# Tail of a decoder layer on one core: routers paired, the last tile's router fed from raw tokens, loads moved to another queue

## The chip, the cores and the metric

The kernel runs on one core of a Trainium2 chip. The metric is the device time of one execution in microseconds (us); the number compared is the median of several runs. TensorE multiplies matrices into PSUM; VectorE (DVE), ScalarE (ACT) and GpSimd (POOL) work elementwise; SyncE (SP) only starts DMA transfers. ScalarE can start DMA transfers as well, from its own queue, and they stand there in order with its other instructions.

## The reference

There are 2048 tokens (32 sequences of 64) of width 512, everything in float32. Three sublayers with residuals:

```python
x = x + attn(layernorm(x))      # 32 heads of 128, RMS norm of q and k, output weights Wo (4096 x 512)
x = x + xattn(layernorm(x))     # 64x64 weights, context of 128 columns, a softmax, and a skip product
x = x + ffn(layernorm(x))
# ffn, with flat = layernorm(x), 64 experts, 8 chosen:
logits = flat @ router_weight.T + router_bias
scores = softmax(logits)
topk_w, topk_idx = top_k(scores, 8)
w_dense = zeros.at[arange(T)[:, None], topk_idx].add(topk_w)
out = flat * topk_w.sum(-1, keepdims=True) + w_dense @ expert_bias
```

## The kernel before, in words

The 2048 tokens are 16 tiles of 128. In a first phase TensorE makes the queries, keys and values of two heads at a time and half of the tokens (32 groups, by a Strassen scheme on two levels), and the mixed values of each group go to DRAM (`mixed`). In the second phase the output product with Wo runs over eight pairs of tiles, again by Strassen: seven products of 32 matmul records each (16 blocks of 128 rows in float32; every record is a 128x256 product). `chunks` (L879) yields after every 4 blocks, that is after 8 records, and after every yield `advance()` runs one step of the work that follows: each tile that has its attention output has a generator `after_attention`, made of `cross_attention` and `experts`, and `yield n` in it lets n further calls of `advance()` pass before its next step. At an `advance()` the tiles take their steps in the order of their numbers. A tile's steps in `cross_attention`: load of the context tile `ct` and layernorm (L1087); `kv` (L1094); the energies `e` and the softmax (L1105 to L1139); the transposes of the probabilities (L279, copies L1144); the skip product (L1114) and the mixtures (L1149), added to x (L1158). In `experts`: layernorm; transposes of the normed tile and a copy to `ft` (L1168); the logits `pl` with `ft` as the stationary operand and the 64 router columns moving (L1173); softmax and choice of eight on VectorE and ScalarE (L1178 to L1205); the weights turned (L1212); the product with the expert biases `pm` (L1222), the last addition (L1225) and the store (L1226). Tiles 2p and 2p+1 already share the turned weights (`wds` of both beside each other); tiles 14 and 15 go alone.

The order on TensorE is the order of the code throughout. On VectorE, ScalarE and GpSimd it is the order of the code up to the end of the first phase (`ordered.close()`), and is planned by the framework after it, from priorities and estimated times. A tile of a pool waits until the buffer of its tag is free; `att` and `ft` have one buffer each.

After the last product TensorE has nothing but tiles 14 and 15 left. There `fill(n)` puts n transposes of the identity into TensorE's queue, after the steps that the table `FILL` names. From the loop over the pairs, pair 7 calls `advance()` a second time behind chunks 8, 12, 16 and 18, and at its end `while tails: advance()` runs the rest.

In the last group of the first phase, a plan of 4 x 4 steps (`plan` in `double`, filled by `also(n, m, ...)`) also holds the first loads of the output product: `load_wo` (L851) with two transfers of 1 MB a call, from SP's queue at the start of the group and from ScalarE's at step (1, 0), and the mixtures of tiles 0 and 1 (L863) at steps (2, 0) to (2, 2). The same queue of SP carries the norms' factors: `row_w` out (L652), `rs` back in as a broadcast (L563), from which `scale` (L574 on VectorE, L572 on GpSimd) works.

Of the kernel before, what the change touches and what calls it, by code (L numbers as in the profile page):

```python
# [41 lines left out]
def decoder_layer(  # L42
# [182 lines left out]
    def fill(count):  # L225
# [8 lines left out]
        (NT - 1, "keys"): 18,  # L234
        (NT - 2, "mixtures"): 18,
# [610 lines left out]
    def load_wo(k, n, places, queue):  # L846

        halves = []
        for i, it in enumerate(places):
            it = it.rearrange("p (g f) -> p g f", f=DH)  # L850
            queue.dma_start(  # L851
                out=it,
                in_=wo.rearrange("(g k p) f -> k p g f", k=HG, p=HD)[
                    k, :, i * KH : (i + 1) * KH, bass.ts(n, DH)
                ],
            )
            halves.append(it)
        return halves
# [225 lines left out]
    def cross_attention(t, xt, apart):  # L1084
# [5 lines left out]
        nc.sync.dma_start(out=ct, in_=ctx_flat[bass.ts(t, P), :])  # L1090
# [27 lines left out]
        py = skip() if t == NT - 1 else None  # L1118
        probs = []
        for b in range(2):  # L1120
# [4 lines left out]
            nc.vector.tensor_scalar(neg, mx, -(SEQ**-0.5), None, ALU.mult)  # L1125
# [20 lines left out]
        yield 2  # L1146
# [12 lines left out]

    chosen_by = {}  # L1160

    def experts(t, xt):
        name = f"f{t}"
        xn = layernorm(xt, name)

        yield 8 if t == NT - 2 else 3
        ft = work.tile([P, KC, P], F32, tag="ft", name=f"ft_{name}", bufs=1)
        nc.scalar.copy(ft, transposed(xn.rearrange("p (kc k) -> p kc k", k=P), name))  # L1168
        fill_behind(t, "router's input")
        yield 1  # L1170
        pl = ps_s.tile([P, NEXP], F32, tag="ps", name=f"pl_{name}")
        for kc in range(KC):
            nc.tensor.matmul(  # L1173
                pl, ft[:, kc, :], rwt[:, kc, :], start=kc == 0, stop=kc == KC - 1
            )
        fill_behind(t, "router")
        lg = work.tile([P, NEXP], F32, tag="lg", name=f"lg_{name}")
        nc.vector.tensor_tensor(lg, pl, rb_b, ALU.add)  # L1178
        top = small.tile([P, 8], F32, tag="top", name=f"top_{name}")
        nc.vector.max(top, lg)  # L1180
        neg = small.tile([P, 1], F32, tag="neg", name=f"neg_{name}")
        nc.vector.tensor_scalar(neg, top[:, 0:1], -1.0, None, ALU.mult)
        ex = work.tile([P, NEXP], F32, tag="ex", name=f"ex_{name}")
        den = small.tile([P, 1], F32, tag="den", name=f"den_{name}")
        nc.scalar.activation(ex, lg, AF.Exp, bias=neg, accum_out=den)
        inv = small.tile([P, 1], F32, tag="inv1", name=f"inv1_{name}")
        nc.vector.reciprocal(inv, den)

        rest = work.tile([P, NEXP], F32, tag="rest", name=f"rest_{name}")
        nc.vector.match_replace(rest, top, lg, -3e38)  # L1190
        chosen = work.tile([P, NEXP], F32, tag="chosen", name=f"chosen_{name}")
        nc.vector.tensor_tensor(chosen, lg, rest, ALU.not_equal)

        alone = t >= NT - 2
        side = 0 if alone else t % 2
        if side:
            wds, other = chosen_by.pop(t - 1)
        else:
            wds = work.tile([P, 2, NEXP], F32, tag="wds", name=f"wds_{name}")
        wd = wds[:, side, :]  # L1200
        nc.vector.scalar_tensor_tensor(wd, ex, inv, chosen, ALU.mult, ALU.mult)
        ws = small.tile([P, 1], F32, tag="ws", name=f"ws_{name}")
        nc.vector.tensor_reduce(ws, wd, AX.X, ALU.add)

        nc.vector.scalar_tensor_tensor(xt, xn, ws, xt, ALU.mult, ALU.add)  # L1205
        if not alone and not side:
            chosen_by[t] = wds, xt
            return
        yield 3
        n = NEXP if alone else 2 * NEXP  # L1210
# [434 lines left out]
```

## Time and profile before

| what | us |
|---|---|
| median of 3 runs | 1870.45 (1868.06 to 1873.12) |
| the profiled execution | 1869.75 |
| its span, first to last instruction | 1868.0 |
| TensorE busy (matmul) | 1850.4 |
| VectorE busy | 1245.1 |
| GpSimd busy | 1014.7 |
| ScalarE busy | 653.6 |
| last product with Wo ends | 1841.1 |
| `fill` in the whole span | 76 transposes |

Times in the timeline count from the first instruction of the span. A group of instructions is given as start, length, engine, line, out<-in and count; "PEld" is the loading of the stationary operand, which overlaps the products. A float32 matmul appears as two records. The granted TensorE clock was 0.999 of full speed over the span.

### The profile page before, as it was taken

Reading aid. Unit: us, or ns where it says so; the run is one execution under the profiler, and the core shown is the slowest. Engines: PE = TensorE matmul, PEld = TensorE weight load, DVE = VectorE, ACT = ScalarE, POOL = GpSimd, SP = SyncE. Lnnn points to the kernel's source line nnn. Section 1 sums busy time; section 2 is a strip of 40 time slices with the busy share of each in tenths; the row PEclk is TensorE's granted clock in tenths of the full one; section 3 lists DMA queues with packets and bytes.
Section 4 is the critical chain, followed back from the end, with each engine's and each line's share of the span. In section 5 each row is a group of like instructions: output and inputs, shape, how many; then the busy total and the mean of one; then the engine's idle time right before and its main releaser. Section 6 shows DMA issues by size and latency. Waiting matters only on the chain.

```text
span 1868.0 us, 40676 instructions
## 1 busy us (share of the span) xinstructions
PE 1850.4 (99%) x16914; PEld 1616.9 (87%) x16914; DVE 1245.1 (67%) x2110; ACT 653.6 (35%) x1577; POOL 1014.7 (54%) x852
## 2 busy tenths in 40 slices
PE   9999999999999999999999999999999999999999
PEld 8888998898899888898889988988888888788876
DVE  6877777777666758777667767766684445554555
ACT  2344444444433443434443343444312202221222
POOL 4866777776667639776667777766242121212120
PEclk9999999999999999999999999999999999999999
DMA  4234434433443343333343333334944231223100
GB/s 143 69 122 144 134 125 131 131 109 110 131 136 114 114 139 112 109 109 103 130 134 123 109 110 114 103 115 141 312 122 159 91 116 68 71 94 116 46 26 23
DMA packets 164650, 215.06 MB, mean 115 GB/s; under 512 B 10161, under 2 KB 135153, under 8 KB 160369
## 3 DMA queue, kind: packets, MB, share of 16 engines
q1 hardware_dynamic: 157648, 206.62, 34.2%
q10 hardware_dynamic: 6816, 5.83, 1.0%
q8 instruction: 133, 2.18, 0.5%
q14 instruction: 53, 0.43, 0.1%
HBM read 172.05 MB, written 40.37 MB: 114 GB/s over the span
## 4 chain that ended last, share of the span: by engine, by line
PE 88%; DVE 4%; DMA 3%; POOL 3%; ACT 1%; issue 1%; SPq 0%; ACTq 0%; POOLq 0%; DVEq 0%
PE p_w L685 32%; PE py L879 17%; PE va L417 11%; PE vb L417 8%; PE o L622 3%; PE s L585 3%; PE ms_w L821 3%; PE pt_p L279 1%; PE pa L475 1%; PE e_x L1105 1%; PE py_x L1149 1%; PE pt_x L279 1%; POOL w L120 1%; PE pl_f L1173 1%; PE py_x L1114 1%; PE pb L475 1%
## 5 line engine op out<-in xcount | busy, mean ns | idle before, releaser
L685 PE MATMUL p_w<-x,w 128*128 128x256 f32 x2940 | 721.1, 382 | 2.5 <-DVE qk L696 1.7
L685 PEld LDWEIGHTS p_w<-x,w 128*128 128x128 f32 x2940 | 521.4, 190 | 59.3 <-DVE qk L696 1.2
L417 PEld LDWEIGHTS va<-w,x 128*128 128x128 f32 x2048 | 268.6, 192 | 13.0
L696 DVE TENSOR_TENSOR qk<-p_w,qk 128x512 f32<-128x512 f32 x360 | 213.1, 599 | 94.6 <-PE p_w L685 92.3
L433 ACT COPY v<-va 128x256 f32<-128x256 f32 x256 | 96.2, 376 | 497.5 <-PE va L417 497.5
L417 PE MATMUL va<-w,x 128*128 128x128 f32 x2048 | 269.9, 275 | 0.0
L709 DVE TENSOR_TENSOR qk<-p_w,qk 128x512 f32<-128x512 f32 x360 | 220.5, 620 | 46.5 <-PE p_w L685 43.1
L120 POOL TENSOR_TENSOR w<-w 128x768 f32<-128x768 f32 x126 | 249.7, 1993 | 2.4
L572 POOL TENSOR_TENSOR qk<-qk,rs 128x512 f32<-128x512 f32 x128 | 173.0, 1352 | 111.8 <-DMA rs<-row_w 99.4
L295 POOL TENSOR_TENSOR prob<-prob,inv 128x512 f32<-128x512 f32 x64 | 79.2, 1237 | 281.5 <-DVE inv L294 278.3
L879 PE MATMUL py<-wo,a 128*128 128x256 f32 x992 | 227.2, 382 | 0.0
L386 ACT ACTIVATE sq<-qk 128x512 f32<-128x512 f32 x256 | 161.4, 631 | 183.6 <-DVE qk L709 64.4
L879 PEld LDWEIGHTS py<-wo,a 128*128 128x128 f32 x992 | 184.1, 190 | 32.9 <-issue 8.6
L417 PEld LDWEIGHTS vb<-w,x 128*128 128x128 f32 x1536 | 201.3, 192 | 9.7
L417 PE MATMUL vb<-w,x 128*128 128x128 f32 x1536 | 202.4, 275 | 0.0
L574 DVE SCALAR_TENSOR_TENSOR qk<-qk,gqk,rs 128x512 f32<-128x512 f32 x128 | 164.7, 1287 | 3.8 <-DMA rs<-row_w 3.5
L879 PE MATMUL py<-wo_t,a 128*128 128x256 f32 x672 | 155.1, 382 | 0.0
L879 PEld LDWEIGHTS py<-wo_t,a 128*128 128x128 f32 x672 | 124.3, 190 | 18.2 <-issue 1.6
L1003 POOL TENSOR_TENSOR x<-x,p 128x256 f32<-128x256 f32 x42 | 42.9, 1043 | 166.7 <-ACT p L1056 72.2
L437 DVE TENSOR_TENSOR v<-vb,v 128x256 f32<-128x256 f32 x192 | 80.9, 421 | 57.0 <-ACT v L433 28.8
L765 POOL TENSOR_TENSOR qk<-qk 128x256 f32<-128x256 f32 x120 | 102.8, 857 | 10.5 <-DVE qk L709 5.8
L287 DVE TENSOR_REDUCE mx<-s 128x8 f32<-128x512 f32 x64 | 44.1, 689 | 85.4 <-PE s L585 85.3
(197 smaller groups left out, 2253.7 us busy)
## 6 DMA issues: line engine op xcount, KB each, us to landing
rs<-row_w SPq DMA_DIRECT2D x120, 512.0 KB
mixed<-ot SPq DMA_DIRECT2D x64, 512.0 KB
a<-mixed SPq DMA_DIRECT2D x32, 1024.0 KB
w<-in_wq_dram SPq DMA_DIRECT2D x64, 256.0 KB
w<-in_wk_dram SPq DMA_DIRECT2D x62, 256.0 KB
w<-in_wv_dram SPq DMA_DIRECT2D x62, 256.0 KB
x<-in_x_dram SPq DMA_DIRECT2D x20, 256.0 KB
rs<-row SPq DMA_DIRECT2D x8, 512.0 KB
```

Source lines behind the costliest of these rows:

```text
L120: on.tensor_tensor(*(it.rearrange("p c j d -> p (c j) d") for it in (out, a, b)), ALU.subtract)
L386: nc.scalar.activation(sq, of, AF.Square)
L417: nc.tensor.matmul(to[:, j, :], left[i][:, c, j, :], right[i][:, c, 2, :], start=first and j == 0 and c == 0, stop=c == 1, skip_group_chec ...
L433: nc.scalar.copy(self.v[h, ab], what)
L437: nc.vector.tensor_tensor(it, what, it, ALU.add)
L572: nc.gpsimd.tensor_tensor(k, k, rk, ALU.mult)
L574: lambda: nc.vector.scalar_tensor_tensor(q, q, gqk, rq, ALU.mult, ALU.mult)
L685: nc.tensor.matmul(bank[:, s, :], self.w.inner[o][i], inner_x[self.half, o][i], start=first and s == 0, stop=True, skip_group_check=True,)
L696: nc.vector.tensor_tensor(to(t, j), bank, add(t, j), ALU.add)
L709: nc.vector.tensor_tensor(to(t, j), bank, to(t, j), ALU.add)
L765: on.tensor_tensor(to, to, what, ALU.add)
L879: nc.tensor.matmul(py, a[:, g, :], b[g // KH][:, g % KH, :], start=n == 0 and g == 0, stop=n == last and g == NHG - 1,)
```

## The change

- Tiles 0 to 13: the even tile makes its `ft` and stops; with the odd tile's the router weights become the stationary operand (64 columns for each of the two tiles, in the two column halves of the array) and the tokens move. The logits of both tiles come out turned, are copied and transposed back, and both tiles' choices are made in one step. `ft` of two tiles lies in one buffer, that of `att`.
- Tile 15: its raw tokens are transposed before the norm's factors are known. The router weights, centred by their column means (`centre`, called by tile 14), take the mean's place, and the logits are multiplied by `rstd`. The copy to `ft` is shared by ScalarE and VectorE, and `xn` is made on GpSimd. The expert weights are not divided by the softmax sum; the factor comes in with the last addition, which is made in two halves, each with its own product and its own store, on SP's and ScalarE's queue.
- Tile 14: its mixtures come one `advance()` earlier (`yield 1`), and with them all its later steps; its x is scaled and added to on GpSimd.
- `FILL`: 18 after tile 15's keys go, 18 after tile 14's mixtures become 2, 22 after tile 15's energies are new.
- Tile 15's negated maxima are made on ScalarE.
- The context tiles of tiles 0 and 1 are loaded from ScalarE's queue.
- The first four Wo loads are issued one by one from ScalarE's queue, at steps (0, 2), (1, 0), (1, 2) and (1, 3) of the last group.

```diff
     FILL = {
-        (NT - 1, "keys"): 18,
-        (NT - 2, "mixtures"): 18,
+        (NT - 2, "mixtures"): 2,
+        (NT - 1, "energies"): 22,
...
-        nc.sync.dma_start(out=ct, in_=ctx_flat[bass.ts(t, P), :])
+        (nc.scalar if t < 2 else nc.sync).dma_start(out=ct, in_=ctx_flat[bass.ts(t, P), :])
...
+        fill_behind(t, "energies")
...
-            nc.vector.tensor_scalar(neg, mx, -(SEQ**-0.5), None, ALU.mult)
+            if t == NT - 1:
+                nc.scalar.mul(neg, mx, -(SEQ**-0.5))
+            else:
+                nc.vector.tensor_scalar(neg, mx, -(SEQ**-0.5), None, ALU.mult)
...
-        yield 2
+        yield 1 if t == NT - 2 else 2
...
+    def centre():
+        mean_of = work.tile([P, P], F32, tag="wt", name="mean_of")
+        nc.gpsimd.memset(mean_of, 1.0 / D)
+        pc = ps_s.tile([P, NEXP], F32, tag="ps", name="pc")
+        for kc in range(KC):
+            nc.tensor.matmul(
+                pc, mean_of, rwt[:, kc, :], start=kc == 0, stop=kc == KC - 1
+            )
+        it = work.tile([P, KC, NEXP], F32, tag="kvs", name="rwc")
+        nc.vector.tensor_tensor(
+            it, rwt, pc.unsqueeze(1).to_broadcast([P, KC, NEXP]), ALU.subtract
+        )
+        centred.append(it)
...
+        if last:
+            pt = transposed(xt.rearrange("p (kc k) -> p kc k", k=P), name)
+            ((mean, rstd),) = statistics([xt], name)
+            xn = work.tile([P, D], F32, tag="xn", name=f"xn_{name}", bufs=3)
+        else:
+            xn = layernorm(xt, name)
+        if t == NT - 2:
+            centre()
...
+            fts = work.tile([P, 2, KC, P], F32, tag="att", name=f"ft_{name}", bufs=1)
...
+        if last:
+            nc.scalar.copy(ft[:, 0:2, :], pt[:, 0:2, :])
+            nc.vector.tensor_copy(ft[:, 2:4, :], pt[:, 2:4, :])
+            nc.gpsimd.tensor_scalar(xn, xt, mean, rstd, ALU.subtract, ALU.mult)
...
+            plt = ps_s.tile([P, P], F32, tag="ps", name=f"plt_{name}")
+            for kc in range(KC):
+                for side in range(2):
+                    nc.tensor.matmul(
+                        plt[side * NEXP : (side + 1) * NEXP, :],
+                        rwt[:, kc, :],
+                        fts[:, side, kc, :],
+                        start=kc == 0,
+                        stop=kc == KC - 1,
+                    )
+            lgt = work.tile([P, P], F32, tag="wt", name=f"lgt_{name}")
+            nc.scalar.copy(lgt, plt)
+            yield 0
+            pl = ps_s.tile([P, 2, NEXP], F32, tag="ps", name=f"pl_{name}")
+            nc.tensor.transpose(pl.rearrange("p a e -> p (a e)"), lgt, ident)
...
+            if t == NT - 2:
+                nc.gpsimd.tensor_scalar(xn_, xn_, ws, None, ALU.mult)
+                nc.gpsimd.tensor_tensor(x_, x_, xn_, ALU.add)
+            else:
+                nc.vector.scalar_tensor_tensor(x_, xn_, ws, x_, ALU.mult, ALU.add)
-        yield 3
+        yield 3 if alone else 2
...
+        if last:
+            for part, queue in (
+                (slice(0, D // 2), nc.sync), (slice(D // 2, D), nc.scalar)
+            ):
+                nc.vector.scalar_tensor_tensor(
+                    xt[:, part], pms[0][:, part], inv, xt[:, part], ALU.mult, ALU.add
+                )
+                queue.dma_start(out=out_flat[bass.ts(t, P), part], in_=xt[:, part])
+            return
...
-                wo_b = [[load_wo(0, 0, four[0:2], nc.sync)], []]
-                also(1, 0, lambda: wo_b[1].append(load_wo(1, 0, four[2:4], nc.scalar)))
+                wo_b = [[[]], [[]]]
+                for i, at in enumerate(((0, 2), (1, 0), (1, 2), (1, 3))):
+                    also(
+                        *at,
+                        lambda i=i: load_wo(
+                            i // 2, 0, four[i : i + 1], nc.scalar, wo_b[i // 2][0]
+                        ),
+                    )
```

## The prediction

> **What bounds the kernel now.** I read the page first (busy times, the chain that ended last), then TensorE's waits, then the chain in order of time around the places that the diff touches, and TensorE's and VectorE's timelines of one middle pair.
>
> ```profile
> PE 1850.4 (99%) x16914; PEld 1616.9 (87%) x16914; DVE 1245.1 (67%) x2110; ACT 653.6 (35%) x1577; POOL 1014.7 (54%) x852
> PE 88%; DVE 4%; DMA 3%; POOL 3%; ACT 1%; issue 1%; SPq 0%; ACTq 0%; POOLq 0%; DVEq 0%
> ```
>
> TensorE is busy for 1850.4 of 1868.0 us. So the time falls only with TensorE work that goes away, with a wait of TensorE that ends, and in the last 27 us, where the two last tiles are a chain across engines and much of "busy PE" is `fill`. TensorE's waits from 1400 us on:
>
> ```profile
> PE kv L1094 <- DMA ct<-in_ctx_dram: 2.2, 1, 2.2
> PE pm_f L1222 <- DVE x L1225: 0.8, 1, 0.8
> ```
>
> Between 100 and 1400 us it waited 4 us in all. One wait is worth an edit: tile 0's context.
>
> **Part 1, the context tiles of tiles 0 and 1 on ScalarE's queue.** The chain in order of time (start, length):
>
> ```profile
> 1401.31 5.33 DMA xw<-in_xwv_t_dram
> ...
> 1407.61 10.38 DMA ct<-in_ctx_dram
> ...
> 1418.13 0.46 PE kv L1094 x2
> ```
>
> The 64 KB load stands on SP's queue behind three 1 MB loads of mixtures (1397.58 to 1407.09) and a 256 KB load of x, and needs 10.38 us. TensorE stops at about 1415.95. On ScalarE's queue it follows the small weight loads, whose last issue ends at 1408.3; ScalarE is idle from then until 1412.34, so two more issues (0.33 us each) hold nothing up. The xw load there landed in 5.33 us, which gives 1408.6 + 5.3 = 1413.9, before 1415.95: 2.2 us gone. A rule speaks against it: the Trainium skill, DMA: Bandwidth & Descriptors, section "Issuing engines are not separate DMA queues", says that transfers of all issuing engines share the same 16 DMA engines, and that a second issuer saves only issue time. By it I would write 0.3 us. I follow the row (5.33 against 10.38 within the same 20 us) and take **-2.2**, with 0 as the other end. Next behind it: product 1 then starts at 1416.4; its a11 was issued before the last of the three large loads, and the DMA engines moved 381 GB/s from 1408 to 1410 and then fell to 121, so that I count it as landed. The sum `a22` for product 5 ends on VectorE at 1421.8, product 5 starts near 1425: covered by 3 us.
>
> **Part 2, paired routers (14 of 16 tiles).** A middle pair on TensorE:
>
> ```profile
> 1765.51 1.00 PE L1173 MATMUL pl_f<-rwt,ft_f 128*128 128x64 f32 x8
> 1766.35 1.95 PE L879 MATMUL py<-wo_t,a 128*128 128x256 f32 x8
> ...
> 1773.31 0.27 PE L1212 MATMUL pw_f<-ident,wds_f 128*128 128x128 f32 x1
> ```
>
> From start to start one router takes 0.84 us, and the chunk behind it 1.78 instead of 1.73: 0.89 a tile, 1.78 a pair. Eight records in 0.84 are 0.105 each, the pitch of a 128-column transpose (8 in 0.87), although only 64 columns move. After: 16 records, the weights 128x64 in alternating column halves, 128 columns moving. Their cost is not in the trace. Upper bound: no overlap, 16 x 0.107 = 1.71. Lower: full overlap, 0.86. Nearest row: L1149 uses column halves of the same kind; its 4 records of 512 columns take 1.01, where L1114's two full ones take 0.86, so 4 cost 59% of 4 full ones: 1.71 x 0.59 = 1.01. What follows a change of array shape also pays:
>
> ```profile
> 1829.93 1.73 PE py L879 x8
> 1831.66 1.09 PE e_x L1105 x16
> 1832.75 1.92 PE py L879 x8
> ```
>
> 0.19 more for the eight records behind e_x. With the new transpose of the logits (0.11): 1.01 + 0.19 + 0.11 = 1.31 a pair, against 1.78: 0.47 saved, times 7 = **-3.3**. The rule here is the Trainium skill, TensorEngine Tiling (Array Packing), "Performance Considerations": with 64 moving columns swap the operands and use two column tiles, up to 2x. By it the pair costs 0.89 + 0.11 and the sum would be -5.5; the 59% and the 0.19 say less. Ends: -5.6 (0.86 + 0.11) and +1.6 (no overlap).
>
> What hides the rest: the logits' copy (about 0.27 us on ScalarE, like wt_f) has a 1.73 us chunk until the transpose asks for it. Then VectorE does both routers in one go. One router's instructions follow at a pitch of 1.66 us to `wds` and 0.9 more for `ws` and x; the second again to `wds` about 1.4 with its waits filled; with the two sums of L1072 and L1073 (0.83) this is 4.0 to 4.9 us. The transposed weights (L1212) are asked for three chunks later, 5.2 us. Slack 0.3 to 1.2 us, less 0.3 of latency: I cost it at nothing, and without cover it is the excess times 7.
>
> The ft tile takes the buffer of `att`; the even tile's copy comes one chunk after the odd tile's mixtures (1753.3, pt_f at 1755.1), so it waits for nothing.
>
> **Part 3, the Wo loads of the last group on ScalarE's queue.** SP loses two 1 MB issues at 1299.02, ScalarE's two at 1315.58 become four: after its v copy (near 1311.5), at 1315.9, after probt (1319.2), and behind the ot copies of `attend` (1326.8). On ScalarE they stand before copies that have 2 to 5 us of idle time in front of them, and the first product wants these weights at 1345. But the bytes move towards a full stretch:
>
> ```profile
> 1310.00:1320.00 10.00, 10.00 (x65) 9.28 (x65) 6.85 (x10) 2.54 (x6) 3.82 (x3) 1.00 0.73 186
> 1320.00:1330.00 10.00, 10.00 (x145) 8.99 (x144) 7.82 (x14) 3.72 (x8) 2.17 (x2) 1.00 1.03 358
> ```
>
> (last two columns: DMA share, GB/s.) By 1320 the old order had issued some 6.8 MB and moved 4.8; the new one leaves about 2.6 MB for later instead of 2.0. That is 0.6 MB / 340 GB/s = 1.8 us, of which some 1 us fits into free shares between 1327 and 1341. So row_w and then rs land about 0.8 us late:
>
> ```profile
> 1344.88 7.92 DMA row_w<-rs_w
> ...
> 1352.94 5.09 DMA rs<-row_w
> ...
> 1358.05 0.04 DVE qk L574
> ```
>
> From there VectorE works without a pause to the wo_t sum of 1376.07, for which TensorE waited; rs late is TensorE late. TensorE has only 0.4 us of waits here to win. Bounds -0.4 and +2; I take **+0.5**.
>
> **Part 4, the end.** The chain there:
>
> ```profile
> 1842.43 1.96 PE fill L230 x18
> 1844.40 1.09 PE e_x L1105 x16
> ...
> 1852.71 1.09 PE py_x L1149 x4
> ...
> 1858.58 1.10 PE pl_f L1173 x8
> ...
> 1863.08 1.14 PE pm_f L1222 x2
> ...
> 1864.24 0.69 DVE x L1225
> ```
>
> I follow TensorE's written order. *Energies of tile 15*: in place of 18 fills stand tile 14's skip (0.86) and mixtures (1.01 + 0.19), 2 fills (0.22) and the new column means of the router's weights (8 records, 0.86): 3.14 instead of 1.96, so e_x starts 1.2 late. *Its softmax*: the negation on ScalarE lets the exponentials start after the first maximum (-0.5), the second negation is 0.2 between them, and VectorE no longer stands in tile 14's addition and statistics when the last sum arrives (-0.45): now 0.45 late. The 22 fills lie inside this. *Mixtures of tile 15*: tile 14's router input now stands ahead, 4 transposes (0.44) and 5 fills (0.55): 1.45 late. *From there to pw of tile 15*, 8.75 us before: x's addition 0.79, transposes of raw x 0.7, tile 14's logits 1.1 (they wait for these transposes in the queue), 15 fills 1.65, wds of 14 0.2, pw and 3 fills 0.45, logits of 15 1.1, 3 fills 0.33, pm of 14 1.1, 8 fills 1.06: 8.5. So the early transpose wins 0.25 and no more, since the last logits stand behind pw of tile 14. *The last additions*: a half of 0.43 for 0.69, and 128 KB on each of two queues instead of 256 KB in the 3.0 us from issue to end: together -0.45. Sum 1.45 - 0.25 - 0.45 = **+0.8** (-1.5 if the means run ahead of need and ScalarE's start gains more; +2 if GpSimd is slow). On GpSimd are new: a memset, tile 15's xn, and two passes over tile 14's x, each near the 1.27 of its 128x512 addition (L867); they lie beside pw and pm, 2.5 us of 2.9. Were they late, tile 14's addition (0.69) would stand before tile 15's on VectorE.
>
> **Sum.** -2.2 - 3.3 + 0.5 + 0.8 = -4.2. The profiled execution was 1869.75 with a span of 1868.0: 1865.5. It lies 0.7 under the median of 1870.45, so as a median **1866.2**.
>
> **Rivals.** *A, faster by more than 0.3%* (0.33): column halves overlap nearly fully (-5), the end gains 1 instead of losing 0.8, Wo costs nothing: -2.2 - 5 - 1 = -8, 1862. For it: L821's four column strips of 256 columns take 0.058 a record, near a quarter of 0.213. Against: e_x with 16 records of 128 columns takes 1.09. *B, slower* (0.10): the doubled router chain on VectorE is late for L1212 in each pair. From 1.4 us of lateness (a chain of 6.6 instead of 4.9) 7 waits eat all of -4.2 plus 5.6; at 2 us it is 7 x 2 - 4.2 = +9.8, 1880. For it: the order on VectorE is a planner's, and large sums of 2.28 us stand there at other times. Against: in a middle pair VectorE is idle 5.6 us before 1775. *C, the context load is late anyway* (within the forecast): x, issued beside it, also landed at 1418; then -2.0, 1868.4. *D, the end does not do what it says*: that is my forecast for it already.
>
> **Chances.** The forecast with C holds 0.57 and is within 0.3% (5.6 us, what a measurement here can tell from no change). The range leaves out a third of A, at its lower end, and B: 1861.0 to 1871.5; the forecast's own is 1864.8 to 1869.
>
> **What would show it.** kv of tile 0 without a DMA wait; 16 plt records in 0.9 to 1.1 us and the chunk behind at 1.92; no wait of pw for wds; rs at 1358.5 to 1359 and s or py waiting for VectorE there; in the end e_x of tile 15 a good microsecond later after pt_x, logits of tile 15 behind pw of 14. I am wrong if pw waits in each pair, if plt takes 1.7, or if the end is shorter by over 1 us.

## The result and the profile after

The changed kernel takes **1876.05 us** (median of 20 runs, 1871.42 to 1881.46) against 1870.40 us for the kernel before in the same comparison (20 runs): ratio **1.0031, interval 1.0024 to 1.0039**. It is 5.7 us slower. The forecast was 1866.2 us, 4.3 us faster; the result lies outside its range and on the other side.

The profiled execution of the changed kernel has a span of 1875.0 us, 7.0 more than before. Three landmarks on TensorE (start of `e_x` of tile 0, start of `pt_x` of tile 14, end of the span) split it:

| stretch | before | after | difference |
|---|---|---|---|
| start to `e_x` of tile 0 | 1422.64 | 1430.01 | +7.4 |
| `e_x` of tile 0 to `pt_x` of tile 14 | 418.31 | 415.21 | -3.1 |
| `pt_x` of tile 14 to the end | 27.05 | 29.78 | +2.7 |

The middle, where the paired routers are, gives what was forecast. Both ends give it back and more. Busy times on the page of the changed kernel, and the chain's shares:

```profile
PE 1847.5 (99%) x16919; PEld 1611.5 (86%) x16919; DVE 1242.3 (66%) x2103; ACT 654.9 (35%) x1586; POOL 1017.3 (54%) x856
PE 89%; DVE 4%; DMA 3%; POOL 2%; ACT 1%; issue 1%; SPq 0%; ACTq 0%; DVEq 0%; POOLq 0%
```

TensorE is busy for 2.9 us less and the span is 7.0 longer, so no work was added: the loss is waiting and, inside the busy time, a lower clock. TensorE's waits between 1300 and 1436 us (total, times, longest), first in the kernel before, then in the changed one:

```profile
PE kv L1094 <- DMA ct<-in_ctx_dram: 2.2, 1, 2.2
PE ms_w L821 <- ACT sq L386: 0.4, 1, 0.4
```

```profile
PE kv L1095 <- DMA ct<-in_ctx_dram: 4.7, 1, 4.7
PE s L585 <- POOL qk L572: 2.8, 1, 2.8
```

The wait for the context tile, which was to go away, went from 2.2 to 4.7 us, and a wait in front of the last group's `s` is new. Then comes something that no wait shows. TensorE's timeline of the changed kernel from the late `kv` on (start, length, in brackets the wait and what ended it):

```profile
1422.52 0.77 PE L1095 MATMUL kv<-ct,wqk 128*128 128x128 f32 x2 [4.75 <-DMA ct<-in_ctx_dram]
...
1423.51 3.62 PE L880 MATMUL py<-wo,a 128*128 128x256 f32 x8
...
1430.01 1.16 PE L1106 MATMUL e_x<-kvs,xn_x 64*128 64x128 f32 x16
```

Eight matmul records of the product take 3.62 us; before, the same eight took 1.89:

```profile
1418.65 1.89 PE L879 MATMUL py<-wo,a 128*128 128x256 f32 x8
```

The table by windows says why (window, length, busy time of TensorE, its weight loads, VectorE, ScalarE, GpSimd; then the granted clock of TensorE, the DMA share, GB/s):

```profile
1420.00:1422.00 2.00, 0.00 (x0) 0.00 (x0) 0.26 (x1) 0.00 (x0) 1.26 (x1) 0.94 1.02 418
1422.00:1424.00 2.00, 1.48 (x6) 1.42 (x7) 2.00 (x2) 0.25 (x1) 0.00 (x0) 0.50 0.77 316
...
1426.00:1428.00 2.00, 2.00 (x8) 1.75 (x7) 0.69 (x1) 0.00 (x0) 0.00 (x0) 0.50 0.00 0
1428.00:1430.00 2.00, 2.00 (x8) 1.40 (x7) 0.00 (x0) 0.37 (x1) 0.00 (x0) 0.85 0.11 33
```

The clock is granted at half for 6.8 us, from 0.75 us before the wait ends. From `kv` to `e_x` of tile 0 it is 7.49 us instead of 4.51: 3.0 us more than the wait itself costs. So the +7.4 are 1.8 (everything behind `rs` is late), 2.6 (4.75 of wait instead of 2.15) and 3.0 (clock).

The late `rs`, in the chain in order of time:

```profile
1346.75 7.96 DMA row_w<-rs_w
...
1354.86 4.99 DMA rs<-row_w
...
1359.87 0.04 DVE qk L574
```

The two transfers take as long as before (7.92 and 5.09); it is `row_w`'s issue that comes 1.87 us later. The paired router in the middle, same view of the changed kernel:

```profile
1470.45 1.02 PE plt_f L1236 x16
1471.47 1.92 PE py L880 x8
1473.40 0.11 PE pl_f L1247
```

The end, same view:

```profile
1852.04 0.55 DVE xn_f L269
1852.59 0.61 DVE mx_x L1125
...
1859.95 1.06 PE py_x L1155 x4
...
1867.83 1.21 DVE chosen_f L1272
...
1870.12 1.14 PE pm_f L1303 x4
...
1871.29 0.48 DVE x L1311
```

The maxima of tile 15 (`mx_x`) start right behind the normed tokens of tile 14 (`xn_f`), although their energies were ready at about 1850.8. Before, they started as soon as the energies ended, at 1845.5 (VectorE's timeline):

```profile
1845.52 1.29 DVE L1123 TENSOR_REDUCE mx_x<-e_x 128x4 f32<-128x512 f32 x2 [1.47 <-PE e_x L1105]
```

### The profile page after: what moved, and what is told of

It is laid out like the page before. It is cut to its first block, busy times and chain, and to the rows that moved or that the text cites. A ratio compares the mean times of both kernels' runs of the same rounds, so it can differ in the third digit from the quotient of the medians.

```text
span 1875.0 us, 40705 instructions
## 1 busy us (share of the span) xinstructions
PE 1847.5 (99%) x16919; PEld 1611.5 (86%) x16919; DVE 1242.3 (66%) x2103; ACT 654.9 (35%) x1586; POOL 1017.3 (54%) x856
## 4 chain that ended last, share of the span: by engine, by line
PE 89%; DVE 4%; DMA 3%; POOL 2%; ACT 1%; issue 1%; SPq 0%; ACTq 0%; DVEq 0%; POOLq 0%
PE p_w L685 33%; PE py L880 18%; PE va L417 11%; PE vb L417 9%; PE o L622 3%; PE s L585 3%; PE ms_w L821 3%; PE pt_p L279 1%; PE pa L475 1%; PE py_x L1155 1%; PE e_x L1106 1%; PE pt_x L279 1%; PE py_x L1115 1%; DMA ct<-in_ctx_dram 1%; PE pb L475 1%
## 5 line engine op out<-in xcount | busy, mean ns | idle before, releaser
L765 POOL TENSOR_TENSOR qk<-qk 128x256 f32<-128x256 f32 x120 | 103.0, 860 | 10.4 <-DVE qk L709 5.7
L637 ACT ACTIVATE ot<-o,bvt 128x256 f32<-128x256 f32 x256 | 99.4, 470 | 2.2 <-PE o L622 2.2
```

The costliest lines, as they stand in the source:

```text
L637: nc.scalar.activation(ot[:, h, :, b * SEQ : (b + 1) * SEQ], o[b][:, h, :, :], AF.Identity, bias=bvt[:, hg * HG + h : hg * HG + h + 1],)
L765: on.tensor_tensor(to, to, what, ALU.add)
```

## The experiments

Sizes in us are the difference of two ratios, each against the kernel before on the same chip, times 1870. "Clock" is the granted clock averaged over all timed runs; for the kernel before it was 0.9985 to 0.9987 on every chip, for the changed kernel 0.9965. A clock lower by 0.001 is at most 1.9 us of the time; it costs nothing where TensorE has no work, as behind its last product.

| run | median | ratio, interval | clock |
|---|---|---|---|
| the change | 1876.05 | 1.0031 [1.0024, 1.0039] | 0.9965 |
| e1_ct: Part 1 alone | 1873.81 | 1.0012 [1.0000, 1.0025] | 0.9982 |
| e2_wo: Part 3 alone | 1871.68 | 1.0013 [1.0006, 1.0019] | 0.9982 |
| e3_pair: Part 2 alone | 1868.65 | 0.9991 [0.9981, 1.0001] | 0.9986 |
| e4_pair_end: Parts 2 and 4 | 1871.94 | 1.0007 [1.0001, 1.0014] | 0.9977 |
| e5_change_early: the change, context early | 1871.77 | 1.0012 [1.0004, 1.0021] | 0.9975 |
| e6_pair_early: Part 2, context early | 1864.82 | 0.9971 [0.9960, 0.9982] | 0.9994 |
| e7_end_order: e4, maxima first | 1867.66 | 0.9987 [0.9981, 0.9994] | 0.9990 |
| e8_end_order_dve: e7, one pass on VectorE | 1867.82 | 0.9991 [0.9984, 0.9999] | 0.9986 |
| e9_change_bo: e5, bias later | 1869.01 | 0.9989 [0.9981, 0.9998] | 0.9981 |
| e10_pair_bo: e6, bias later | 1865.51 | 0.9965 [0.9952, 0.9977] | 0.9986 |
| e11_pair_wo_bo: e10 with Part 3 | 1865.79 | 0.9969 [0.9959, 0.9978] | 0.9987 |
| e12_repaired: the change, four losses mended | 1865.62 | 0.9969 [0.9957, 0.9980] | 0.9990 |
| e13_change_fill: the change, transposes in the wait | 1879.01 | 1.0048 [1.0032, 1.0064] | 0.9955 |
| e15_pair_wo: e6 with Part 3 | 1868.83 | 0.9990 [0.9983, 0.9996] | 0.9979 |
| e14_pair_wo_row: e15, row_w on ScalarE's queue | 1865.67 | 0.9976 [0.9965, 0.9987] | 0.9991 |
| e16_pair_row: e6, row_w on ScalarE's queue | 1867.00 | 0.9980 [0.9971, 0.9989] | 0.9990 |
| e17_ct_late: e14, context as in the change | 1873.73 | 1.0008 [0.9994, 1.0021] | 0.9973 |
| e18_ct_late_fill: e17, transposes in the wait | 1872.97 | 1.0005 [0.9995, 1.0015] | 0.9984 |

### Which part loses

Each part alone on the kernel before, and the end on top of the pairing. The edits are the change's own hunks; the one for Part 1 is

```diff
-        nc.sync.dma_start(out=ct, in_=ctx_flat[bass.ts(t, P), :])
+        (nc.scalar if t < 2 else nc.sync).dma_start(out=ct, in_=ctx_flat[bass.ts(t, P), :])
```

and for Part 3

```diff
-                wo_b = [[load_wo(0, 0, four[0:2], nc.sync)], []]
-                also(1, 0, lambda: wo_b[1].append(load_wo(1, 0, four[2:4], nc.scalar)))
+                wo_b = [[[]], [[]]]
+                for i, at in enumerate(((0, 2), (1, 0), (1, 2), (1, 3))):
+                    also(
+                        *at,
+                        lambda i=i: load_wo(
+                            i // 2, 0, four[i : i + 1], nc.scalar, wo_b[i // 2][0]
+                        ),
+                    )
```

Part 1 alone:

> Part 1 alone on the kernel before: only the two context loads go to ScalarE's queue. The prediction: tile 0's kv waits for nothing, 2.2 us less, ratio 0.9988. What the changed kernel's trace suggests: the load is issued behind the small weight loads and lands no earlier than before; TensorE waits 2 to 5 us,[...] so the run is equal or up to 5 us longer.

Part 3 alone:

> Part 3 alone: only the first four Wo loads go one by one to ScalarE's queue. The prediction: rs lands about 0.8 us late, +0.5 in all. From the changed kernel's trace: the wait of 1.0 us for the squares near 1342 goes, because the two issues of step (3, 1) take 1.0 instead of 2.6 us, but rs lands 1.8 us later than before and s waits 2.8 us, so +0.8 to +1.8 us at the end of the first phase; the context load, later by as much, adds nothing to that or pulls TensorE into a wait above 3 us.

Part 2 alone:

> Part 2 alone: only the routers of tiles 0 to 13 are paired. The prediction and the trace of the changed kernel agree: from the first energies to the end of the last product 3.3 us less, nothing else moves; ratio 0.998 to 0.9985. The rival (pw of a pair waits for the doubled router chain): no gain or a loss, with a wait of pw for wds in each pair.

Parts 2 and 4:

> Parts 2 and 4: paired routers and the new end, both sets of loads as before. The prediction: -3.3 + 0.8, 2.5 us less than before. From the changed kernel's trace the end costs 2.9 us, because VectorE takes tile 14's normed tile ahead of tile 15's maxima: against the run with the paired routers alone +2.9, against the kernel before -0.4.

Measured: Part 1 +2.2 (interval 0 to +4.7), Part 3 +2.4 (+1.1 to +3.6), Part 2 -1.7 (-3.6 to +0.2), Part 4 (e4 against e3) +3.0, give or take 2.2. Their sum is 5.9, the change as a whole 5.8: with such intervals so close an agreement is luck. Parts 3 and 4 lose clearly, Part 1 at the edge of its interval. Part 2's place in the profile, from `e_x` of tile 0 to `pt_x` of tile 14, is 415.14 us in both of its runs against 418.31: -3.2, without the scatter of the rest. Part 4's is the end: 29.88 us against 27.04, +2.8, with the waits of the changed kernel. The loads are harder to read in one execution: the profiled one of Part 1 alone (1868.62 us; its ten runs go from 1868.60 to 1875.78) shows no wait in front of `kv` at all, as forecast, because the context landed 6.8 us after its issue; that of Part 3 alone shows 2.35 us in front of `s`.

### The context tiles

In the change they stand on ScalarE's queue behind the router's weights. The changed kernel's issues there, ScalarE's queue:

```profile
1409.49 1.85 ACTq L221 DMA_DIRECT2D eb_sb<-in_eb_dram  x2
1411.38 1.50 ACTq L1091 DMA_DIRECT2D ct<-in_ctx_dram  x2
```

The small loads ahead of them take until 1411.34 to issue, and the tile lands 11.0 us later. So the place was moved: the tiles are allocated and issued first on that queue when the output phase opens.

```diff
-        ct = work.tile([P, MCTX], F32, tag="ct", name=f"ct_{t}")
-        (nc.scalar if t < 2 else nc.sync).dma_start(out=ct, in_=ctx_flat[bass.ts(t, P), :])
+        if t < 2:
+            ct = ct_first[t]
+        else:
+            ct = work.tile([P, MCTX], F32, tag="ct", name=f"ct_{t}")
+            nc.sync.dma_start(out=ct, in_=ctx_flat[bass.ts(t, P), :])
...
+    ct_first = [work.tile([P, MCTX], F32, tag="ct", name=f"ct_{t}") for t in range(2)]
+    for t in range(2):
+        load_beside(ct_first[t], ctx_flat[bass.ts(t, P), :])
     bo_b = work.tile([P, D], F32, tag="bo", name="bo_b", bufs=1)
```

> The whole change, with the context tiles of tiles 0 and 1 issued first on ScalarE's queue in the output phase, ahead of the router's weights, instead of behind them. Theory (the loss of Part 1 is the late landing, and the clock that halves behind the wait): TensorE's wait in front of kv falls from 4.7 us to under 0.5, the granted clock stays at 1.00 through the first mixtures, and e_x of tile 0 starts 5 to 7 us earlier than in the change: 1869 to 1871.5 us. Rival (the context tiles land when the mixtures' big loads are through, wherever they are issued): the wait stays at 2 us or more and the time at 1874 to 1877.

The context tile is issued at 1397.40, before the three 1 MB loads of mixtures, and lands 1.9 us later (by the DMA's completion records in the trace). The wait in front of `kv` is gone and the clock there is 1.00; the change gains 3.6 us (1871.77, 0.3 above the theory's range). The rival is out. What was left shows in the windows of its profiled execution, where the clock now falls in two other places:

```profile
1368.00:1370.00 2.00, 1.58 (x52) 1.51 (x56) 2.00 (x1) 0.00 (x0) 2.00 (x2) 0.80 0.30 78
1370.00:1372.00 2.00, 2.00 (x50) 1.79 (x44) 1.90 (x4) 0.00 (x0) 1.64 (x1) 0.50 0.54 197
...
1848.00:1850.00 2.00, 0.63 (x4) 0.42 (x4) 1.23 (x3) 1.89 (x9) 0.00 (x0) 1.00 0.00 0
1850.00:1852.00 2.00, 1.57 (x8) 1.60 (x9) 0.28 (x1) 0.53 (x2) 0.00 (x0) 0.62 0.00 0
1852.00:1854.00 2.00, 2.00 (x12) 2.00 (x11) 0.00 (x0) 0.10 (x1) 0.00 (x0) 0.53 0.00 0
```

One stands behind the wait in front of `s` (3.00 us here), one behind the waits of the new end. Without those two parts:

> The kernel before with the paired routers (Part 2) and the early context tiles; Wo's loads and the end as before. Theory: the pairing's 3.2 us and the 1.9 to 2.2 us of the wait in front of kv add up: 1865 to 1867 us, a ratio of 0.997 to 0.998. Rival (the context tiles' landing doesn't depend on their place in the queue, or their issue pushes other loads late): 1868 to 1870, as the pairing alone.

1864.82 us, 0.2 below the theory's range, with the highest mean clock of all runs. This version beats both kernels.

### The end

The written order of VectorE is made by the planner. VectorE's timeline of the changed kernel:

```profile
1850.88 0.18 DVE L256 BATCH_NORM_AGGREGATE mv_f<-st_f 128x2 f32<-128x6 f32 x1
1852.04 0.55 DVE L269 TENSOR_SCALAR xn_f<-x,mv_f,rs_f 128x512 f32<-128x512 f32 x1 [0.98 <-POOL rs_f L260]
1852.50 1.28 DVE L1125 TENSOR_REDUCE mx_x<-e_x 128x4 f32<-128x512 f32 x2
```

It waits 0.98 us for a root from GpSimd in order to norm tile 14, with tile 15's maxima queued behind. The next run starts from Parts 2 and 4 (e4) and moves that step one advance later:

```diff
-        (NT - 1, "energies"): 22,
+        (NT - 1, "energies"): 14,
...
+            if t == NT - 2:
+                yield 0
             xn = layernorm(xt, name)
...
-        yield 8 if t == NT - 2 else 3
+        yield 7 if t == NT - 2 else 3
```

> Pairing and the new end, loads as before, with tile 14's layernorm step one advance of its generator later and the planner's energies of the last tile due earlier, so that VectorE's order has the maxima of tile 15 ahead of tile 14's normed tokens. Theory (the new end lost its time because the maxima stood behind VectorE's wait for GpSimd): the end from tile 14's transposes to the end of the span falls from 29.7 us to 27.2 to 27.8, and the time from 1871.9 to 1869.3 to 1870. Rival (the mixtures of tile 14 and the halves are what costs): the end stays at 29 or more and the time within 0.7 us of 1871.9.

VectorE's timeline of that run now has them the other way round, with no wait between:

```profile
1842.94 1.25 DVE L1125 TENSOR_REDUCE mx_x<-e_x 128x4 f32<-128x512 f32 x2
1844.11 0.54 DVE L269 TENSOR_SCALAR xn_f<-x,mv_f,rs_f 128x512 f32<-128x512 f32 x1
```

The end is 27.54 us instead of 29.88, as expected, and the time falls by 3.7 us, more than the 1.9 to 2.6 expected; the mean clock is higher by 0.0013, which goes the same way. Most of the end's loss was the order, not the mixtures of tile 14 or the halves. In the same run VectorE's last selection still takes 1.22 us while GpSimd adds tile 14's gated tokens. The next run gives these additions back to VectorE:

```diff
-            if t == NT - 2:
+            if False:
                 nc.gpsimd.tensor_scalar(xn_, xn_, ws, None, ALU.mult)
```

> As the run with the changed order in the end, and in addition tile 14's gated additions as one pass on VectorE instead of two halves on GpSimd. Theory (VectorE's last selection took 1.21 us instead of 0.22 because GpSimd worked beside it): the selection is back at about 0.2 us, TensorE's last mixture starts up to 1 us earlier, and the time is 0.3 to 1 us below the run beside it. Rival (the extra pass on VectorE stands in the way of the last tile's own steps): the time is 0.3 us or more above it.

The selection takes 0.23 us and the end 27.15, both as expected, but the time is the same (0.9991 against 0.9987, intervals overlap): 0.4 us can't be told in the time of the whole kernel.

### Part 3 and the output bias

The changed kernel's issues on SP's queue:

```profile
1339.38 1.99 SPq L852 DMA_DIRECT2D wo<-in_wo_dram  x2
1341.46 5.20 SPq L217 DMA_DIRECT2D bo<-in_bo_dram  x1
1346.75 1.15 SPq L652 DMA_DIRECT2D row_w<-rs_w  x2
```

ScalarE had the roots at 1343.94, so `row_w` lost 2.8 us behind the issue of the output bias, which is first used some 55 us later. Before, the roots ended at 1344.86, when the bias's issue had just ended:

```profile
1340.76 4.03 SPq L217 DMA_DIRECT2D bo<-in_bo_dram  x1
1344.88 1.15 SPq L652 DMA_DIRECT2D row_w<-rs_w  x2
```

So the slow issue is not new; with Part 3 it starts 0.7 us later and takes longer, while the roots come earlier. With the old loads it also took 5.88 and 5.11 us in two other profiled executions (e3, e6), where TensorE waited 1.6 and 0.4 us in front of `s`. The first attempt moves the bias behind `row_w`:

```diff
-    load(bo_b, bo.partition_broadcast(P))
     wo_t = four_blocks("wo_t")
...
         line.turn()
         go(3)
         line.scale()
+        load(bo_b, bo.partition_broadcast(P))
```

> The change with the early context tiles, and in addition the load of the output bias for the first tiles (whose issue took 4 to 6 us on SP's queue) issued behind the last head group's row_w and its first root loads instead of ahead of them; it is first used 50 us later. Theory (Part 3 loses because row_w stands behind that issue, so that rs comes late, TensorE waits 2.4 to 3.0 us in front of s and its clock sometimes halves there): row_w is issued about 3 us earlier, the wait in front of the second group of s falls under 0.5 us, and the time from 1871.8 to 1867.5 to 1869.5 us. Rival (rs is late for another reason, the latency of the two DMAs): the wait stays over 2 us and the time within 0.7 us of 1871.8.

> Paired routers, early context tiles and the output bias's load moved; Wo's loads and the end as before. Theory: with the old loads of Wo the wait in front of s was 0.3 to 1.6 us, so this gains that and no more: 1863.3 to 1864.6 us beside the 1864.8 without the move. Rival (the bias's load in its new place holds up the last root load or the tiles of x): over 1865.5.

> As the run before it, with the change's loads of Wo (four pieces, two of them issued on ScalarE's queue in 1.0 us). Theory (Part 3 on its own makes the mean squares start and end some 1 us earlier, and only row_w's place took it back): 0.5 to 1.2 us below the run before it, 1862.3 to 1864. Rival (the four pieces cost something of themselves): 0.5 us or more above it.

> The whole change with each loss mended: early context tiles, the bias's load moved, tile 15's maxima ahead of tile 14's normed tokens, tile 14's additions on VectorE. Only the new end sets it apart from the pairing with the change's Wo loads. Theory (the new end, mended, is worth nothing: 27.15 us against 27.05): within 0.7 us of that run, 1862.3 to 1864.7. Rival (its two longer waits of TensorE in the last tile still let the clock halve in some executions): 1 us or more above it, with a mean granted clock lower by 0.0005 or more.

The first time is in the theory's range (1869.01); the others, 1865.5 to 1865.8, lie 0.9 to 1.8 us above theirs (e10 at the edge of its rival), on a chip where the kernel before took 1.5 us more than in the runs they were set against. But the mechanism did not come out. In the profile of the first, the load that took the bias's place, x, took 5.80 us to issue, `row_w` stood behind it as long as ever (6.6 us after the mean squares' start, as in the change), and the wait in front of `s` was 2.57 us. With Part 3 but otherwise mended (e11, e12) it was 0.91 and 1.65 us. So it is not the bias as such: the load that follows Wo's on SP's queue is slow to issue (3.6 to 6.0 us in the profiled executions), whichever it is. That Part 3 gains, as the third theory said, is not confirmed (0.9969 against 0.9965), and the mended end cannot be told from the old one (0.9969 both). Whether the bias's move gains by itself is open: e10 and e6 overlap.

That left the cause open, so Part 3 was put alone on the paired kernel with early context, and `row_w` then moved off SP's queue:

```diff
-        nc.sync.dma_start(out=row, in_=rs.rearrange("(s r) a n -> s r a n", r=32)[:, 0, :, :])
+        last = name.endswith(f"w{NHEAD // HG - 1}_1")
+        (nc.scalar if last else nc.sync).dma_start(out=row, in_=rs.rearrange("(s r) a n -> s r a n", r=32)[:, 0, :, :])
```

> Paired routers and early context tiles, with the change's loads of Wo (Part 3) and no other move: set against 1864.8 us without Part 3. Theory (mean squares 1 us earlier, but row_w 1.5 to 3 us later behind SP's next load, whose issue takes 5 us): between 0.3 us better and 1.7 us worse, 1864.5 to 1866.5, with TensorE's wait in front of s at 2 us or more. Rival (Part 3 gains): under 1864.2.

> As the run before it, with the last head group's two row_w transfers issued on ScalarE's queue, which made the roots, instead of SP's. Theory (row_w stands behind an issue that SP's queue can't finish while Wo's loads drain): row_w is issued within 0.3 us of the roots, some 2 to 4 us earlier, the wait in front of s falls under 0.7 us, and the time is 1 to 2.5 us below the run before it. Rival (on ScalarE's queue the issue is held up as long, or the transfer itself, 7 to 8 us among Wo's packets, sets the landing): within 0.7 us of the run before it, or above.

> Paired routers, early context tiles, Wo's loads as before, row_w on ScalarE's queue. Theory: there row_w was issued on SP within 0.1 to 1 us of the roots, so little is gained: within 0.7 us of 1864.8. Rival (ScalarE's place for the issue delays its own exponentials, which set TensorE's next step): 1866 or more.

Part 3 costs 3.6 us there (0.9990 against 0.9971; 1868.83 us, 2.3 above the theory's range), and its profile has the wait, from 1366.0 to 1369.1, and the clock halved from there to 1372.7. TensorE's waits from 1340 to 1376 us in that run:

```profile
PE s L585 <- POOL qk L572: 3.1, 1, 3.1
```

and with `row_w` on ScalarE's queue:

```profile
PE pt_p L279 <- POOL prob L295: 0.9, 1, 0.9
```

`row_w` is issued at 1343.82, right behind the roots, instead of 1346.91, the wait in front of `s` is gone, and 2.6 us come back, give or take 2.4 (1 to 2.5 expected). So `row_w`'s place on SP's queue is what makes Part 3 lose, or most of it. The new wait of 0.9 us is the price: the issues of 1.08 and 0.50 us stand ahead of ScalarE's own exponentials. With Wo's loads as before the move gains nothing: the median, 1867.00, is on the rival's side, the ratios (0.9980 against 0.9971) overlap, so whether it loses there is open.

### The clock behind the wait

Does the clock fall because TensorE stood idle? Thirty transposes of the identity, whose result the next matmul overwrites, are put into the wait:

```diff
         kv = ps_s.tile([P, 2, MCTX], F32, tag="ps", name=f"kv_{t}")
+        if t == 0:
+            for _ in range(30):
+                nc.tensor.transpose(kv[:, 0, :], ident, ident)
```

> The change as it is, with thirty idle transposes (0.11 us each, 3.3 us, overwritten by what follows) issued on TensorE in front of kv of tile 0, inside the 4.75 us in which it waits for the context tile. Nothing else is moved, and kv can start no earlier. Theory (behind the wait the clock halves because TensorE stood idle, and that costs 3 us more than the wait itself): the granted clock stays at 1.00 through the first mixtures, e_x of tile 0 comes some 4.4 us after kv's start instead of 7.4, and the time falls by 1.7 to 3.5 us, from 1876.05 to 1872.5 to 1874.3. Rival (the clock falls there for another reason, or the transposes only delay kv): 1875.5 or more.

In the profiled execution `kv` still waited 1.03 us behind the transposes, the clock stayed at 1.00 throughout, and `kv` to `e_x` took 5.05 us instead of 7.49: at this spot it is as the theory said. The time is on the rival's side: 1879.01 us in only four runs, with a wait of 4.0 us in front of `s` in the profiled one, and a clock halved behind that wait (1370 to 1377) and twice more. So few runs, each with further halvings, do not settle the total. The pair was repeated without the wait in front of `s`:

> The paired routers, the change's loads of Wo, row_w on ScalarE's queue (so that no wait stands in front of s), the end as before, and the context tiles of tiles 0 and 1 behind the router's weights as the change has them: apart from their place it is the run of 1865.7 us that had row_w on ScalarE's queue. Theory: TensorE waits 4 to 6 us in front of kv and the clock halves behind it, which costs wait and clock: 1870.5 to 1874. Rival (with s on time the context tiles land early enough, or the wait is made up later): within 1.5 us of 1865.7.

> As the run before it, with the thirty idle transposes (3.3 us) inside the wait in front of kv of tile 0. Theory (the clock halves because TensorE stood idle): no halved clock at the first mixtures, mean granted clock higher by 0.001 to 0.002, and the time 1.5 to 3 us below the run before it. Rival (the transposes spare the clock there but leave a halving for later, as the run with them in the change may show): within 0.7 us of the run before it, with the mean granted clock the same within 0.0005.

TensorE's timeline without transposes,

```profile
1426.05 0.46 PE L1096 MATMUL kv<-ct,wqk 128*128 128x128 f32 x2 [4.13 <-DMA ct<-in_ctx_dram]
...
1426.57 3.01 PE L881 MATMUL py<-wo,a 128*128 128x256 f32 x8
```

and with them:

```profile
1418.38 3.44 PE L1098 MATMUL kv<-ident 128*128 128x128 f32 x30
...
1422.11 1.89 PE L881 MATMUL py<-wo,a 128*128 128x256 f32 x8
```

With the late context the kernel loses 6.0 us (1.0008 against 0.9976), in the range expected. Not all of that is the context's: the profiled execution also waits 5.0 us for the probabilities near 1350 (0.9 in e14), with a halving of its own, because `row_w`'s second issue on ScalarE's queue comes late; so does the one with transposes (2.8 us). With the transposes the mean clock rises by 0.0011, give or take 0.0009, as the theory said; that is worth at most 2.1 us. The time falls by 0.6 us, not by 1.5 to 3, and the intervals overlap. The second profiled execution shows nothing of a filled wait: by the DMA's completion records in its trace the context had landed at 1418.1, before the transposes began, so all of their 3.3 us was cost. That filling the wait pays is not shown; loading earlier does (e5).

What decides whether a wait halves the clock? The traces hold the moment of every change of the granted clock. Within one execution the halvings begin on a grid of 3.413 us: with the early context (e5) at 1369.20, 1850.48 and 1867.54, which are 141 and 5 steps apart, and in the changed kernel at 1421.77 and 1872.33, 132 steps apart. The grid lies elsewhere in each execution. Every window of the grid in all 20 traces, from 20 us to TensorE's last product, was taken with the share of it in which TensorE was busy. All 11 windows with a share of 0.40 or less were followed by half clock. Of the 10,779 others seven were: two that ran at half clock themselves, and five around one pair of thin products (below). The windows of the grid around the wait in front of `s`, in e5 and in the changed kernel (columns as above):

```profile
1365.78:1369.20 3.42, 0.78 (x24) 0.78 (x24) 3.42 (x3) 0.00 (x0) 3.42 (x3) 1.00 0.02 5
1369.20:1372.61 3.41, 3.41 (x73) 2.97 (x68) 2.94 (x4) 0.34 (x1) 2.44 (x1) 0.50 0.48 156
```

```profile
1363.75:1367.16 3.41, 2.25 (x17) 1.62 (x15) 3.41 (x4) 0.00 (x0) 2.77 (x2) 1.00 0.18 53
1367.16:1370.57 3.41, 1.81 (x88) 1.74 (x88) 3.41 (x2) 0.00 (x0) 3.41 (x2) 1.00 0.23 65
```

A wait of 3.00 us nearly all in one window leaves TensorE 0.78 us of work there, and the next window runs at half clock. One of 2.76 us that is shared by two windows leaves it 2.25 and 1.81, and neither is followed by half clock. So it is idleness that halves the clock, counted by window; the length of a wait alone does not decide. With the transposes in the change's wait (e13) TensorE was busy for 2.38 of the 3.41 us of the window with the wait that was left, and the clock stayed.

## Why the prediction was wrong

From the forecast of -4.2 us to the measured +5.8 it is 10.0. In the parts' own times Part 1 makes 4.4 of it, Part 4 2.2, Part 3 1.9 and Part 2 1.6.

**Part 1 (forecast -2.2, measured +2.2).** Two steps failed. The first is "The xw load there landed in 5.33 us, which gives 1408.6 + 5.3 = 1413.9". In the change the context came behind four more loads than that xw, was issued at 1411.38 instead of 1408.6 (1.8 us of this is the late `rs`), and took 11.0 us. From this place it took 6.7 to 11.3 us in five profiled executions (the change, e1, e13, e17, e18), on SP's queue 7.9 to 10.4 in six, by the completion records in the traces. So a second issuer brought no reliably faster landing, and the rule that was weighed and set aside (the Trainium skill, DMA: Bandwidth & Descriptors, "Issuing engines are not separate DMA queues") was the better guide. What makes the landing vary from one execution to the next stays open. The second step is missing from the forecast altogether: a wait can cost more than its length. 4.75 us of wait cost 3.0 us more in clock.

**Part 2 (forecast -3.3, measured -3.2 in its stretch, -1.7 in the time, whose interval of about 2 us either way takes in both).** Right by each term on TensorE: the sixteen records take 1.02 us (1.01 forecast), the chunk behind them 1.92 (1.73 + 0.19), the logits' transpose 0.11. No wait for `pw` appeared in the pairs. The rule's -5.5 was too much.

**Part 3 (forecast +0.5, measured +2.4 alone, +3.6 beside the pairing).** The direction was right and `rs` was the right carrier, the reason was not, so the sign came out by luck. The failed step is "That is 0.6 MB / 340 GB/s = 1.8 us", which made `rs` late by bytes still to move. In the profile the two transfers take as long as before, the roots are even 0.9 us earlier, and `row_w` is late because SP could not issue it: 5.2 us go by in the issue of the load in front (4.0 before), which also starts 0.7 us later. What stands in front of an issue and behind it was read for ScalarE's queue and not for SP's, though the wait in front of `s` and the clock behind it follow from there.

**Part 4 (forecast +0.8, measured +2.8 in the end, +3.0 in the time).** Counted from `pt_x` of tile 14, the energies of tile 15 start 4.49 us later, before 3.38: 1.1 late, 1.2 forecast. Its second transposes of probabilities start after 12.46 instead of 10.48 us: 2.0 late, 0.45 forecast. So the failed term is the softmax, "-0.5" and "-0.45": it let VectorE take the maxima when the energies were there. The planner had put tile 14's normed tokens, and with them a wait for GpSimd, ahead. Tile 14's router input in front of the mixtures adds 1.0 us, as forecast: they start after 14.73 instead of 11.76 us, 3.0 late, 1.45 forecast. From there to the end it is 15.05 instead of 15.29: -0.2, -0.7 forecast. What failed there is the "-0.45" for the last additions: the two halves take 0.88 us together where one addition took 0.69, and the end comes 2.9 us behind them instead of 3.0. With the order mended (e7) the mixtures start after 12.39 us, 0.6 late, and the end is 27.54, +0.5 where +0.8 was forecast. In three other profiled executions with the new end as it was (e5, e9, e13) its two waits of 1.7 and 1.0 us fell into one window of the clock's grid, the clock halved behind them and the end took 31.2 to 31.5 us.

**The clock over all runs.** The changed kernel's mean clock is 0.9965. That of the kernel before, in the runs beside the first four experiments, is 0.9986: (0.9986 - 0.9965) x 1870 = 3.9 us at most, since half clock behind TensorE's last product costs nothing (2.7 us of it in the profiled execution of the change). In that execution 3.0 of the 7.0 us are the clock, in one place. The sum of the forecast had no term for this. Rival C (context late anyway) named the place, but with Part 1 at nothing instead of +2.2, and rival B, the one meant for a slower result, did not occur.

## What to carry to other kernels

Where a wait of TensorE can leave it busy for 0.4 or less of a window of 3.4 us, cost the half clock behind it too, up to 1.7 us for each window, and look for the load or the order that ends the wait before filling it. Where the windows lie cannot be known beforehand, so it is a chance and not a sum. When an issue is moved to another queue, read the issue times of everything that stands in front of it there, and what the queue that it left now issues late. Where a planner writes the order of an engine, compare the new order with the old one before costing a step at the time its inputs are ready.

## What was not expected of the hardware

**The clock follows waits that are short.** In the profiled executions it was halved behind single waits of 2.80, 3.0, 3.1, 4.0, 4.1, 4.75 and 5.0 us, for 3.41 us or twice that, and stayed at 1.00 behind 2.15, 2.35, 2.57 and 2.76 us. The Trainium skill, TensorE: Matmul & The Clock Gate, Part 1, gives a free-running activity window of about 3.4 us, with half rate after an idle one. The grid of 3.413 us agrees; but the window need not be idle here, a busy share of up to 0.40 was enough. What the busy share does not explain is a wait of 0.78 us between two gated mixtures (`pm_f`) of an early pair: a window of the grid that held the whole of it was busy for 0.77, and in 5 of 17 executions the clock halved behind it (e2, e6, e10, e12, e13). Windows of the paired kernel with early context (e6),

```profile
1476.00:1478.00 2.00, 1.22 (x3) 0.38 (x3) 1.02 (x3) 2.00 (x13) 0.00 (x0) 1.00 0.00 0
1478.00:1480.00 2.00, 2.00 (x5) 1.08 (x4) 1.83 (x4) 0.33 (x2) 0.00 (x0) 0.69 0.35 131
1480.00:1482.00 2.00, 2.00 (x6) 1.55 (x6) 0.00 (x0) 0.00 (x0) 0.00 (x0) 0.50 0.55 188
```

where the kernel before, with the same two mixtures and its wait between them, kept 1.00 in its profiled execution. What sets the five apart is open. A halving of 3.41 us costs up to 1.7, which may be much of the scatter between runs of one kernel: of the 53 runs of the kernel before beside the first four experiments, the 23 with a granted clock of 0.999 took 1869.6 us on average, the 20 with 0.998 1871.2 and the three with 0.997 1873.4.

**An issue can take 4 to 6 us, whichever load it is.** Behind Wo's loads the next load on SP's queue took 5.20 us (bias, 256 KB, in the change; 4.03 before) or 5.80 (x, 256 KB, in e9), and a load of x took 0.33 to 0.39 us in other places of the two kernels. What holds it was not looked into.

**A small VectorE operation took 1.22 us instead of 0.23 beside GpSimd's addition.** In the run with the mended order (e7), VectorE's and GpSimd's timelines:

```profile
1858.23 1.22 DVE L1274 TENSOR_TENSOR chosen_f<-lg_f,rest_f 128x64 f32<-128x64 f32 x1
```

```profile
1858.09 1.28 POOL L1289 TENSOR_TENSOR x<-x,xn_f 128x512 f32<-128x512 f32 x1
```

The selection starts after the addition's start and ends within 0.1 us of it; with the addition on VectorE (e8) it took 0.23 us. The Trainium skill, SBUF — State Buffer, "SBUF: two separate sides", says that an operation of VectorE with two inputs in SBUF and one of GpSimd that reads SBUF share a pair of ports which one of them holds until it has ended; this pair of rows agrees. The forecast had placed these passes of GpSimd beside `pw` and `pm` and not asked what they do to VectorE.
